# Two layers of attention on one core: v from seven block products in place of eight, and additions moved to transfers

## The chip, the cores and the metric

The kernel runs on one core of a Trainium2 chip. The core has five engines that each work through a list of their own: TensorE (PE: matrix products into PSUM), VectorE (DVE), ScalarE (ACT), GpSimd (POOL) and SyncE (SP, which only issues transfers here). They wait for each other through semaphores. The measure is the device time of one execution in microseconds (us), and lower is better.

## The reference

The reference takes 16 samples x of 256 channels by 1024 positions (32 x 32) through two layers. Each layer normalises in 16 groups and adds an attention with 4 heads of 64 channels to its input. Cut to what matters:

```python
for l in range(2):
    xf = group_norm(x)                        # per sample: (256, 1024)
    q, k, v = (W @ xf + b for W, b in ...)    # 256 x 256 weights
    sim = q_head.T @ k_head                   # (1024, 1024) for each head
    qpos = (rel_h + rel_w).T @ q_head
    attn = softmax(sim + qpos, axis=-1)
    x = x + v_head @ attn.T
```

## The kernel before

**Units and blocks.** One sample in one layer is a unit. There are 32, in the order of the list `units`, u = 0 to 31. A unit has four blocks, b = 0 to 3: pair of heads pr = 0 with query half 0 and 1, then pair pr = 1 with half 0 and 1. Blocks 0 and 2 are called the first and the second even block here, 1 and 3 the odd ones. `block(n)` writes out the program of block n. Everything is recorded in this order (`tc.manual_schedule`), and each engine works strictly through its own part of it, so a statement's place in `block` sets the order on every engine.

**One block.** For each of eight chunks j of 128 keys: `seed(blk, j)` lets VectorE write the position term of both heads into two PSUM banks (128 x 1024 values, L513; with `halves` it is two instructions of 512). `scores(blk, j)` adds q k on TensorE (S1 to S7 below are the scores of chunk 1 to 7; L549, four matmuls of 512 columns) and ScalarE takes exp into an SBUF tile p (L562). `attend` multiplies v by all eight p (L602) in two passes, called `values_of_p(0)` and `(1)`, with the first scores of the next block in between. `add_up` adds the p of a block up for the softmax's denominator: p0 + p1 is `first`, p2 comes to it by an accumulating transfer, the rest goes into `acc`. Transfers from POOL's queue with `accum_op` then fold the sums (`add_first`, `fold`, `fold_again`, `fold_stack`).

**The array.** Every large matmul uses one 64 x 64 quarter of TensorE's array. A stage has work for all four quarters at once, and comes as two stretches (`stretches`): the second adds the other half of the contraction and waits until the first is done. Each fp32 matmul shows up as two records in the trace. A round means one record on each of the four quarters.

**Banks.** PSUM's eight banks are used as four pairs, named by `ring`: ta, tb, tx, tz. In an even block tz holds q and k under construction (`qk`), and ta, tb, tx serve the seeds. tx first holds v under construction (`pv`, two stretches of 32 records), is copied out by ScalarE after S2 (`v_out`, L470) and then takes seeds; the output `po` sits in tx at the block's end.

**q, k, v.** While the blocks of one pair of heads run, q and k of the next pair (w, pr) are made: with seven products of 128 x 128 by 128 x 512 blocks in place of eight (Strassen's scheme in Winograd's form). `forms` makes the sums of weight blocks S1 to S4, `input_sums` those of the input T1 to T4 (L344, L349, L351, in a second even block). The first product stands alone (`first_product`, L360) and is woven with the first stretch of v (`woven`), since each of its stretches uses half of the array. The other six come as three pairs (`two_products`, L409). v itself is made with all eight block products, one half of the positions in each even block (`values`, L445; matmuls of 256 columns).

**The end of a block.** Six blocks later `finish` multiplies the output by 1/denominator (`normalise`, L720) and adds the bias of v and the residual (`add_residual`, L727), both on VectorE; in layer 1 SP stores the result. The norm of later units is spread over ScalarE by tables (`APPLY`, `NEXT`, `SUMS`, `SQUARES`: at which point of block b which of the 16 groups are done; L221, L296).

Of the kernel before, what the change touches and what calls it, by code (L numbers as in the profile page):

```python
# [17 lines left out]
P = 128  # L18
HALF = 512
G = 16  # L20
# [38 lines left out]
def fast_path(ctx, tc, sh, x, layers, out, W, den_all, good, flag):  # L59
# [90 lines left out]

    def taken(parts):
        for l, part in parts:
            w = {"Wq": W.form[l][:, :CC], "Wk": raw_wk(l), "Wv": W.wv[l]}[part]
            nc.scalar.copy(w.rearrange("p a c -> p (a c)"), raw_t.pop((l, part)))

    def forms(l):
# [3 lines left out]
        for to, a, b, op in (  # L160
            (S1, k0, k1, ALU.add),
            (S2, f[:, S1], f[:, A11], ALU.subtract),
            (S3, f[:, A11], k0, ALU.subtract),
            (S4, f[:, A12], f[:, S2], ALU.subtract),
# [271 lines left out]

    def values(u, g, pv, first=None):
# [4 lines left out]
        def part(t, i, cc, rs, a):  # L442
            for x, c in enumerate(QUARTERS):
# [4 lines left out]
                    W.wv[l][rs, cc, :],  # L448
# [245 lines left out]
    def reciprocals(u, pr, count=2):  # L694
# [9 lines left out]
        rden = opool.tile([P, 2 * HALF], F32, tag="rden", name=f"rden_{u}_{pr}")  # L704
# [26 lines left out]
    def add_by_dma(u, pr):  # L731
        b, l = units[u]
        xs = xt[b][:, pr, :]
        nc.scalar.activation(xs, xs, AF.Identity, bias=W.bv[l][:, pr : pr + 1])
        nc.gpsimd.dma_start(xs, outs.pop((u, pr)).rearrange("p a n -> p (a n)"), accum_op=ALU.add)

# [42 lines left out]
    APPLY = {0: (3, 7, 7, 7, 7, 7), 1: (7, 7, 7, 11, G, G)}  # L779
    NEXT = {3: (0, 0, 0, 0, 3, 3)}  # L780
    SUMS = {0: (0, 0, 0, 6, 9, 14), 1: (14, 14, 14, G, G, G)}
    SQUARES = {2: (0, 4, 5, 10, 12, G)}

    FIRST_SQUARES = {0: (2, 5, 9, 12, 12, 12)}
    FIRST_SUMS = {0: (0, 0, 0, 0, 6, 12), }
    FIRST_APPLY = {1: (0, 0, 3, 8, G, G)}

    def norms(u, b, i):
        def groups(table):
            return range(*table.get(b, (0,) * 6)[i : i + 2])  # L790
# [12 lines left out]
    def block(n):  # L803
# [18 lines left out]
        if previous and even:  # L822
            add_up(previous, 7)
        if folded and even:
            add_first(previous)
        if summed:
            fold_stack(*summed, R // 4)
        if even:
            qk = psum2(tz, f"qk_{w}_{pr}") if not plain else None
            first = None if plain else first_product(w, pr, qk)  # L830
            v, v_out = values(w, 1 - b // 2, psum2(tx, f"pv_{w}_{b}"), first)
            if n > 0:
                scores(blk, 1)
            if b == 2:
                input_sums(w, 0)
            v(0)
            norms(u, b, 0)
            if n > 0:
                seed(blk, 3, ta)
# [10 lines left out]
            add_up(blk, 1)  # L850
            v(1)
            if folded:
# [6 lines left out]
            v_out()  # L859
            if n > 0:  # L860
                scores(blk, 3)
            seed(blk, 4, tb)
            if n == 0:
                forms(0)
            if plain:
# [5 lines left out]
            products(0)  # L871
            norms(u, b, 1)
            seed(blk, 5, tx, halves=True)
# [714 lines left out]
```

## Time and profile before

| | us |
|---|---|
| time, median of 3 runs (lowest to highest) | 2478.74 (2478.73 to 2479.44) |
| the profiled execution's own time | 2479.26 |
| its span in the trace | 2477.5 |
| seeds, L513, busy | 1241.2 |
| scores, L549, busy | 1068.9 |
| attention, L602, busy | 951.6 |
| v, L445, busy | 301.3 |

The profile comes from one execution. Each row of a timeline has the start and the length in us from the span's start, the engine, the line and the operation, what is written from what, the shape, how many instructions are merged, and in brackets how long the engine had been idle and what released it. Matmuls are pipelined: the length of a row on PE reaches past the start of the next, so a stage is measured from its start to the next one's start. Rows of groups give the sum of busy time, the mean of one instruction in ns, and the idle time ahead of them. The granted clock of TensorE was 0.999 over the span.

### The profile page before, as it was taken

The page shows a single profiled execution, that of the slowest core. Times are in us where ns is not written, and L with a number is a line of the kernel's source. Part 1 is how long each engine was busy: PE and PEld are TensorE (multiplying, and loading weights), DVE is VectorE, ACT ScalarE, POOL GpSimd, SP SyncE. Part 2 cuts the span into 40 slices and gives each one's busy share as a digit, 9 for nine tenths or more (in the row PEclk, how much of TensorE's full clock was granted, in tenths as well). Part 3 has the DMA queues.
Part 4 walks back from the last instruction along what each step waited for, and adds up shares of the span by engine and source line. Part 5 has one row for each costly group of instructions (what it writes and reads, how often), then busy time and mean ns, then how long its engine had stood idle before and what let it go on. Part 6 is the DMA issues. An engine that isn't in the chain of part 4 may idle for free.

```text
span 2477.5 us, 86516 instructions
## 1 busy us (share of the span) xinstructions
PE 2467.9 (100%) x37030; PEld 1825.8 (74%) x37030; DVE 2350.6 (95%) x2815; ACT 2076.5 (84%) x4341; POOL 795.7 (32%) x942
## 2 busy tenths in 40 slices
PE   9999999999999999999999999999999999999998
PEld 5777777777777777777777777777777777777785
DVE  8899999999999999999999999999999999999998
ACT  8888888898888888888888889888888888888764
POOL 0233333333333333333333333333333333333231
PEclk9999999999999999999999999999999999999999
DMA  3655655657557566565575665665656656556564
GB/s 95 115 104 98 129 96 114 119 118 144 112 115 144 105 116 118 108 137 112 113 133 108 125 119 99 130 134 109 129 118 135 116 93 131 112 96 121 106 129 116
DMA packets 138551, 289.25 MB, mean 117 GB/s; under 512 B 55848, under 2 KB 57384, under 8 KB 138160
## 3 DMA queue, kind: packets, MB, share of 16 engines
q0 software_dynamic: 72288, 197.74, 47.3%
q1 hardware_dynamic: 65584, 85.38, 11.6%
q8 instruction: 293, 4.80, 0.8%
q14 instruction: 98, 0.80, 0.1%
q10 hardware_dynamic: 288, 0.52, 0.1%
HBM read 51.78 MB, written 17.30 MB: 28 GB/s over the span
## 4 chain that ended last, share of the span: by engine, by line
PE 98%; DVE 1%; ACT 1%; DMA 0%; issue 0%; SPq 0%; PEldq 0%; ACTq 0%
PE banks L549 36%; PE banks L602 35%; PE banks L409 13%; PE banks L445 9%; PE banks L486 2%; PE banks L360 2%; PE banks L317 0%; PE banks L240 0%; DVE banks L513 0%; DMA x<-in_x_dram 0%; ACT p L562 0%; PE banks L675 0%; ACT xn L296 0%; ACT junk L221 0%; DVE r L1121 0%
## 5 line engine op out<-in xcount | busy, mean ns | idle before, releaser
L513 DVE TENSOR_TENSOR banks<-abt 128x1024 f32<-128x1024 f32 x1207 | 1241.2, 1061 | 93.3 <-ACT p L562 49.2
L562 ACT ACTIVATE p<-banks,shift 128x1024 f32<-128x1024 f32 x898 | 981.4, 1116 | 202.5 <-PE banks L549 104.6
L549 PE MATMUL banks<-q,k 64*64 64x512 f32 x8192 | 1068.9, 590 | 0.5 <-DVE banks L513 0.4
L602 PE MATMUL banks<-p,v 64*64 64x256 f32 x16384 | 951.6, 376 | 0.0
L602 PEld LDWEIGHTS banks<-p,v 64*64 64x64 f32 x16384 | 838.5, 133 | 120.4 <-issue 39.1
L549 PEld LDWEIGHTS banks<-q,k 64*64 64x64 f32 x8192 | 466.2, 133 | 281.8 <-issue 153.7
L582 DVE TENSOR_TENSOR acc<-acc,p 128x1024 f32<-128x1024 f32 x381 | 465.2, 1221 | 4.3
L648 POOL DMA_DIRECT2D stack<-stack x310 | 308.2, 994 | 316.8 <-DMA stack<-stack 148.7
L409 PE MATMUL banks<-t,form 64*64 64x512 f32 x1984 | 399.7, 589 | 0.0
L643 POOL DMA_DIRECT2D stack<-acc x248 | 241.6, 1186 | 471.2 <-DMA stack<-acc 458.0
L445 PE MATMUL banks<-Wv,xn 64*64 64x256 f32 x3968 | 293.5, 378 | 0.0
L409 PE MATMUL banks<-xn,form 64*64 64x512 f32 x992 | 258.8, 589 | 0.0
L445 PEld LDWEIGHTS banks<-Wv,xn 64*64 64x64 f32 x3968 | 228.9, 133 | 40.2 <-PEq L199 16.8
L619 POOL DMA_DIRECT2D acc<-first x126 | 115.1, 914 | 423.1 <-DVE acc L582 224.3
L296 ACT ACTIVATE xn<-x,nshift,rstd 128x128 f32<-128x128 f32 x496 | 209.3, 500 | 30.1 <-DVE nshift L289 30.1
L221 ACT ACTIVATE junk<-x,neg 128x128 f32<-128x128 f32 x501 | 199.7, 407 | 0.0
L560 ACT ACTIVATE p<-banks,shift 128x512 f32<-128x512 f32 x252 | 159.8, 685 | 35.3 <-PE banks L549 32.3
L409 PEld LDWEIGHTS banks<-t,form 64*64 64x64 f32 x1984 | 137.8, 133 | 67.8 <-issue 41.8
L624 POOL DMA_DIRECT2D acc<-acc x124 | 103.3, 833 | 254.5 <-DMA acc<-first 251.4
L578 POOL DMA_DIRECT2D first<-p x127 | 114.1, 899 | 179.2 <-ACT abt L499 66.8
L567 DVE TENSOR_TENSOR acc<-p,p 128x1024 f32<-128x1024 f32 x128 | 156.2, 1220 | 0.4 <-DMA acc<-first 0.4
L567 DVE TENSOR_TENSOR first<-p,p 128x1024 f32<-128x1024 f32 x127 | 154.7, 1218 | 0.0
(120 smaller groups left out, 1776.6 us busy)
## 6 DMA issues: line engine op xcount, KB each, us to landing
first<-p POOLq DMA_DIRECT2D x127, 512.0 KB, 6.8
acc<-first POOLq DMA_DIRECT2D x126, 512.0 KB, 5.5
rden<-rd SPq DMA_DIRECT2D x126, 256.0 KB, 6.7
acc<-acc POOLq DMA_DIRECT2D x124, 256.0 KB, 5.9
stack<-acc SPq DMA_DIRECT2D x248, 64.0 KB, 2.9
stack<-acc POOLq DMA_DIRECT2D x248, 64.0 KB, 3.4
out_dram<-x SPq DMA_DIRECT2D x31, 512.0 KB, 2.9
x<-in_x_dram SPq DMA_DIRECT2D x30, 512.0 KB, 9.5
```

What stands on the lines that cost most here:

```text
L221: nc.scalar.activation(junk, grouped(xt[units[u][0]], g), func, accum_out=into[:, g : g + 1], **bias)
L296: nc.scalar.activation(grouped(xns[u], g), grouped(xt[units[u][0]], g), AF.Identity, bias=shift[:, g : g + 1], scale=rstd[:, g : g + 1],)
L409: yield nc.tensor.matmul(ps[c, a, :], f[rs, left[a], c0 : c0 + D], right[a][rs, :], start=(t == 0 and step == 1 and a == 1), stop=(t == 1) ...
L445: yield nc.tensor.matmul(pv[c, a, i, :], xns[u][rs, cc, j0 : j0 + D], W.wv[l][rs, cc, :], start=(t == 0 and cc == 0 and i == 0), stop=(t = ...
L513: nc.vector.tensor_tensor(ps[:, h].rearrange("p h (w y) -> p h w y", y=H), ab[:, h, :H].unsqueeze(2).to_broadcast(shape), ab[:, h, H + hal ...
L549: nc.tensor.matmul(ps[c, h, :], a[hs, j0 : j0 + D], b[hs, columns], start=bool(tag) and i == 0, stop=i == len(terms) - 1, skip_group_check ...
L562: nc.scalar.activation(p, ps, AF.Exp, bias=W.shift)
L567: nc.vector.tensor_tensor(t, probs[blk, a], probs[blk, b], ALU.add)
L582: nc.vector.tensor_tensor(accs[blk], accs[blk], probs[blk, j], ALU.add)
L602: yield nc.tensor.matmul(po[c, a, :QUART], vts[u, j // 4][rs, j % 4, c0 : c0 + D], p[rs, h, a * QUART : (a + 1) * QUART], start=(fresh and ...
L643: nc.gpsimd.dma_start(at, acc[R:D, h, :], accum_op=ALU.add)
L648: nc.gpsimd.dma_start(stack[:rows_], stack[rows_ : 2 * rows_], accum_op=ALU.add)
```

## The change

v is made with the seven products too, of weight forms that `value_forms` prepares. Its matmuls have 128 columns (`value_part`), with the input as the stationary operand. It takes three steps in two blocks. The second even block of the unit before has the first product, together with the first product of q and k (`odd_products`: each takes the half of the array that the other leaves free), and a pair (`value_pair`, step 0). The first even block of the unit itself has the two other pairs, the first of them woven with the first product of q and k. v's four blocks are put together from the banks (`bank_of(pv, a)` is one of the two, `value_block` 4 x 128 columns of v): by ScalarE's copies (c22, c11, u2 and a part), by three additions on VectorE (c22, c11, c12), and by two accumulating transfers (c22 += u2, u2 += part) on POOL's queue.

`pv` therefore keeps the pair tx until both steps are done. Seeds 3 to 6 turn on ta and tb, seed 7 goes to tx, and `po` to ta. The bias of v is added to x by ScalarE in block 3 (`add_bias`), and the residual by an accumulating transfer (`add_output`). Some additions of p, and the norm's pieces, have other places.

The first place is the first even block of a unit. PE there, before, from S2 to S7 and the attention, in the block of unit 13, pair 0, half 0 (L549 scores, L445 v, L409 pairs of products, L602 attention; the names are those of the tiles, with unit, pair, half and chunk).

```order
L549 MATMUL banks_127<-q_13_0_12239,k_13_0_12240 64x512 x4
L445 MATMUL banks_127<-Wv1_79,xn_13_11648 64x256 x16
L549 MATMUL banks_127<-q_13_0_12239,k_13_0_12240 64x512 x4
L409 MATMUL banks_127<-t_13_12162,form1_77 64x512 x2
L409 MATMUL banks_127<-xn_13_11648,form1_77 64x512 x2
L549 MATMUL banks_127<-q_13_0_12239,k_13_0_12240 64x512 x8
L409 MATMUL banks_127<-xn_13_11648,form1_77 64x512 x2
L409 MATMUL banks_127<-t_13_12162,form1_77 64x512 x2
L549 MATMUL banks_127<-q_13_0_12239,k_13_0_12240 64x512 x8
```

And now, from S2 to the start of v's third stretch (L630 scores, L457 v, L426 pairs of products):

```order
L630 MATMUL banks_127<-q_13_0_12895,k_13_0_12896 64x512 x4
L457 MATMUL banks_127<-vform1_79,t_13_12837 64x128 x16
L630 MATMUL banks_127<-q_13_0_12895,k_13_0_12896 64x512 x4
L426 MATMUL banks_127<-t_13_12837,form1_77 64x512 x2
L426 MATMUL banks_127<-xn_13_12294,form1_77 64x512 x2
L630 MATMUL banks_127<-q_13_0_12895,k_13_0_12896 64x512 x4
L457 MATMUL banks_127<-vform1_79,xn_13_12294 64x128 x2
L457 MATMUL banks_127<-vform1_79,t_13_12837 64x128 x2
```

v's matmuls are half as wide, and a third stretch of v (eight such rows) has come in behind S4. Behind it follow S5, v's fourth stretch, S6, the stretch of products that stood behind S5 before, and S7.

VectorE in the same block before, from the last addition of the block ahead to the residual (L582 and L567 additions of p, L513 seeds, L720 normalise, L727 the residual):

```order
L582 TENSOR_TENSOR acc_12_1_1_12514<-acc_12_1_1_12514,p_12_1_1_7_12478 128x1024
L513 TENSOR_TENSOR banks_127<-abt_13_0_12512 128x1024
L567 TENSOR_TENSOR first_13_0_0_12668<-p_13_0_0_0_12558,p_13_0_0_1_12633 128x1024
L513 TENSOR_TENSOR banks_127<-abt_13_0_12512 128x1024
L513 TENSOR_TENSOR banks_127<-abt_13_0_12512 128x512 x2
L513 TENSOR_TENSOR banks_127<-abt_13_0_12512 128x1024
L513 TENSOR_TENSOR banks_127<-abt_13_0_12512 128x512 x2
L720 TENSOR_TENSOR od_11_1_11467<-od_11_1_11467,rden_11_1_12461 128x1024
L727 SCALAR_TENSOR_TENSOR x_4_3665<-od_11_1_11467,bv1_85,x_4_3665 128x1024
```

And now (L594 seeds, L663 and L648 additions of p, L972 and L1016 additions for v, L806 normalise):

```order
L663 TENSOR_TENSOR acc_12_1_1_13213<-acc_12_1_1_13213,p_12_1_1_6_13167 128x1024
L594 TENSOR_TENSOR banks_127<-abt_13_0_13211 128x1024
L663 TENSOR_TENSOR acc_12_1_1_13213<-acc_12_1_1_13213,p_12_1_1_7_13177 128x1024
L594 TENSOR_TENSOR banks_127<-abt_13_0_13211 128x1024
L594 TENSOR_TENSOR banks_127<-abt_13_0_13211 128x512 x2
L972 TENSOR_TENSOR v_13_1_13327<-v_13_1_13327,banks_127 128x4x128
L594 TENSOR_TENSOR banks_127<-abt_13_0_13211 128x512 x2
L594 TENSOR_TENSOR banks_127<-abt_13_0_13211 128x1024
L1016 TENSOR_TENSOR v_13_1_13327<-v_13_0_12875,banks_127 128x4x128
L594 TENSOR_TENSOR banks_127<-abt_13_0_13211 128x512 x2
L648 TENSOR_TENSOR first_13_0_0_13476<-p_13_0_0_0_13256,p_13_0_0_1_13332 128x1024
L806 TENSOR_TENSOR od_11_1_12111<-od_11_1_12111,rden_11_1_13160 128x1024
```

Seed 4 is split, the additions for c22 and c12 stand between the seeds, p0 + p1 has moved behind seed 7, and the residual has gone.

The second place is the way from an even block into the odd one. VectorE before, from p3 + p4 of the second even block to the addition of p7 in the odd one (L433 adds into k):

```order
L567 TENSOR_TENSOR acc_13_1_0_13289<-p_13_1_0_3_13175,p_13_1_0_4_13192 128x1024
L582 TENSOR_TENSOR acc_13_1_0_13289<-acc_13_1_0_13289,p_13_1_0_5_13202 128x1024
L513 TENSOR_TENSOR banks_127<-abt_13_1_12982 128x1024
L582 TENSOR_TENSOR acc_13_1_0_13289<-acc_13_1_0_13289,p_13_1_0_6_13216 128x1024
L513 TENSOR_TENSOR banks_127<-abt_13_1_12982 128x1024 x2
L433 SCALAR_TENSOR_TENSOR k_14_0_13179<-banks_127,bk0_82,k_14_0_13179 128x512
L513 TENSOR_TENSOR banks_127<-abt_13_1_12982 128x512 x2
L513 TENSOR_TENSOR banks_127<-abt_13_1_12982 128x1024 x2
L582 TENSOR_TENSOR acc_13_1_0_13289<-acc_13_1_0_13289,p_13_1_0_7_13224 128x1024
```

And now (L450 adds into k):

```order
L648 TENSOR_TENSOR acc_13_1_0_14042<-p_13_1_0_3_13886,p_13_1_0_4_13914 128x1024
L663 TENSOR_TENSOR acc_13_1_0_14042<-acc_13_1_0_14042,p_13_1_0_5_13949 128x1024
L594 TENSOR_TENSOR banks_127<-abt_13_1_13712 128x1024
L663 TENSOR_TENSOR acc_13_1_0_14042<-acc_13_1_0_14042,p_13_1_0_6_13966 128x1024
L663 TENSOR_TENSOR acc_13_1_0_14042<-acc_13_1_0_14042,p_13_1_0_7_13977 128x1024
L594 TENSOR_TENSOR banks_127<-abt_13_1_13712 128x1024 x2
L450 SCALAR_TENSOR_TENSOR k_14_0_13891<-banks_127,bk0_82,k_14_0_13891 128x512
L594 TENSOR_TENSOR banks_127<-abt_13_1_13712 128x512 x2
L594 TENSOR_TENSOR banks_127<-abt_13_1_13712 128x1024 x2
```

The addition of p7 stands ahead of the seed of chunk 3 and not behind that of chunk 7.

ScalarE in the first odd block before, from the copy of k to the exp of chunk 5 (L560 and L562 exp):

```order
L428 COPY k_13_1_12706<-banks_127 128x512
L560 ACTIVATE p_13_0_1_2_12887<-banks_127,shift_71 128x512 x2
L562 ACTIVATE p_13_0_1_3_12895<-banks_127,shift_71 128x1024
L562 ACTIVATE p_13_0_1_4_12903<-banks_127,shift_71 128x1024
L562 ACTIVATE p_13_0_1_5_12914<-banks_127,shift_71 128x1024
```

And now (L641 and L643 exp, L238 a group's sum for the norm):

```order
L445 COPY k_13_1_13404<-banks_127 128x512
L641 ACTIVATE p_13_0_1_2_13612<-banks_127,shift_71 128x512 x2
L238 ACTIVATE junk_15_4_13616,red_15_13557<-x_6_7816 128x128
L643 ACTIVATE p_13_0_1_3_13622<-banks_127,shift_71 128x1024
L643 ACTIVATE p_13_0_1_4_13630<-banks_127,shift_71 128x1024
L643 ACTIVATE p_13_0_1_5_13641<-banks_127,shift_71 128x1024
```

One group's sum stands between the exp of chunk 2 and that of chunk 3.

The diff, cut to what was spoken of. Left out are the same rotation in the program's first and last blocks, the path that is taken only when a denominator leaves its range, `value_forms` (the sums of weight blocks for v), and the places of weights and of 1/denominator in memory.

```diff
+    def value_part(u, ps, rs, a, form, right, i, start=False, stop=False):
+        for x, c in enumerate(QUARTERS):
+            p0 = i * P + x * D
+            yield nc.tensor.matmul(
+                ps[c, a, i * P : (i + 1) * P], right[rs, p0 : p0 + D],
+                W.vform[units[u][1]][rs, form, :],
+                start=start and i == 0, stop=stop, skip_group_check=True,
+            )
+
+    def odd_products(u, pr, qk, pv):
...
+        def products(t):
+            mine, other = ((LO, HI), (HI, LO))[t]
+            for i in range(NT // 2):
+                if i < 2:
+                    c, c0 = QUARTERS[i], pr * P + i * D
+                    yield nc.tensor.matmul(
+                        qk[c, 0, :], f[other, A11, c0 : c0 + D], xb(u, 0, 0)[other, :],
+                        start=t == 0, stop=t == 1, skip_group_check=True,
+                    )
+                yield from value_part(u, pv, mine, 0, A11, xb(u, 0, 0), i, t == 0, t == 1)
+
+        return stretches(products)
+
+    def value_pair(u, step, pv, first=None):
...
+        left, right = (
+            ((S2, A12), (ts[u][:, T2], xb(u, 1, 0))),
+            ((S1, S3), (ts[u][:, T1], ts[u][:, T3])),
+            ((S4, NA22), (xb(u, 1, 1), ts[u][:, T4])),
+        )[step]
+
+        fresh = (1, 0, 2)[step]
...
+        def products(t):
+            rounds = [
+                [
+                    value_part(
+                        u, pv, rs, a, left[a], right[a], i, t == 0 and a >= fresh, t == 1
+                    )
+                    for rs, a in BANKS[t]
+                ]
+                for i in range(NT // 2)
+            ]
+            if t == 0 and first is not None:
+                yield from woven(rounds, first)
+            else:
+                for r in rounds:
+                    for p in r:
+                        yield from p
...
+    def add_bias(u, pr):
         b, l = units[u]
         xs = xt[b][:, pr, :]
         nc.scalar.activation(xs, xs, AF.Identity, bias=W.bv[l][:, pr : pr + 1])
+
+    def add_output(u, pr):
+        xs = xt[units[u][0]][:, pr, :]
         nc.gpsimd.dma_start(xs, outs.pop((u, pr)).rearrange("p a n -> p (a n)"), accum_op=ALU.add)
...
-    APPLY = {0: (3, 7, 7, 7, 7, 7), 1: (7, 7, 7, 11, G, G)}
-    NEXT = {3: (0, 0, 0, 0, 3, 3)}
-    SUMS = {0: (0, 0, 0, 6, 9, 14), 1: (14, 14, 14, G, G, G)}
-    SQUARES = {2: (0, 4, 5, 10, 12, G)}
-
-    FIRST_SQUARES = {0: (2, 5, 9, 12, 12, 12)}
-    FIRST_SUMS = {0: (0, 0, 0, 0, 6, 12), }
-    FIRST_APPLY = {1: (0, 0, 3, 8, G, G)}
+    APPLY = {0: (3, 3, 4, 5, 5, 9, 12, 12), 1: (12, 12, 12, 12, G)}
+    NEXT = {3: (0, 0, 0, 0, 3)}
+    SUMS = {0: (0, 0, 0, 0, 0, 0, 0, 4), 1: (4, 5, 7, G, G)}
+    SQUARES = {2: (0, 0, 1, 2, 4, 8, 11, G)}
...
+        def rest_of_previous():
             add_up(previous, 7)
-        if folded and even:
-            add_first(previous)
+            if folded:
+                add_first(previous)
+
+        if even and b == 2:
+            rest_of_previous()
+            input_sums(w, 0)
...
-            first = None if plain else first_product(w, pr, qk)
-            v, v_out = values(w, 1 - b // 2, psum2(tx, f"pv_{w}_{b}"), first)
+            pv = psum2(tx, f"pv_{w}_{b}")
+            if plain:
+                v, v_out = values(w, 1, pv)
+            elif b == 0:
+                new_values(w, 1)
+                v = value_pair(w, 1, pv, first_product(w, pr, qk))
+            else:
+                v = odd_products(w, pr, qk, pv)
...
-            if not plain:
+            if n > 0:
+                if b == 0:
+                    rest_of_previous()
+                seed(blk, 3, ta)
...
-                scores(blk, 2)
+                scores(blk, 2, halves=b == 0)
...
-            add_up(blk, 1)
             v(1)
+            if b == 2:
+                new_values(w, 0)
+                nc.scalar.copy(value_block(w, 0, 0), bank_of(pv, 0))
+                after_first(w, pr, qk)
+            elif plain:
+                v_out()
+            else:
+                c22, u2 = value_block(w, 1, 1), value_block(w, 0, 1)
+                nc.scalar.copy(c22, bank_of(pv, 0))
...
-            v_out()
+            seed(blk, 4, tb, halves=b == 0 and n > 0)
+            if b == 0 and not plain:
+                nc.vector.tensor_tensor(c22, c22, bank_of(pv, 1), ALU.add)
+                nc.gpsimd.dma_start(c22, u2, accum_op=ALU.add)
...
-            seed(blk, 4, tb)
+            norms(u, b, 1)
...
-            products(0)
-            norms(u, b, 1)
-            seed(blk, 5, tx, halves=True)
-            scores(blk, 4, halves=True)
-            seed(blk, 6, ta)
+                v = value_pair(w, 2 - b, pv)
+            seed(blk, 5, ta, halves=True)
+            if b == 2:
+                v(0)
+                scores(blk, 4)
+                norms(u, b, 2)
+                v(1)
+                c11 = value_block(w, 0, 0)
+                nc.vector.tensor_tensor(c11, c11, bank_of(pv, 1), ALU.add)
+                nc.scalar.copy(value_block(w, 0, 1), bank_of(pv, 0))
+                products(0)
+                norms(u, b, 3)
+                scores(blk, 5)
+                seed(blk, 6, tb)
+                products(1)
+            else:
+                products(0)
+                scores(blk, 4)
+                norms(u, b, 2)
+                if not plain:
+                    v(0)
+                scores(blk, 5)
+                seed(blk, 6, tb)
+                if not plain:
+                    v(1)
+                    c12 = value_block(w, 1, 0)
+                    part = bank_of(xns[w][:, :, :HALF], 0)
+                    nc.scalar.copy(part, bank_of(pv, 1))
+                    nc.vector.tensor_tensor(c12, u2, bank_of(pv, 0), ALU.add)
+                norms(u, b, 3)
             if folded:
                 stack_up(previous)
-            scores(blk, 5)
-            products(1)
-            po = psum2(tx, f"po_{n}")
+            po = psum2(ta, f"po_{n}")
             zeroed(po)
-            seed(blk, 7, tb, halves=True)
+            seed(blk, 7, tx, halves=True)
             scores(blk, 6)
+            if b == 0:
...
+            if not plain:
+                add_up(blk, 1)
             if before:
-                finish(*before)
+                normalise(*before)
+                add_output(*before)
+                if units[before[0]][1] == NL - 1:
+                    store(*before)
...
+            ta, tb, tx = tb, tx, ta
+            ring[:] = ta, tb, tx, tz
             seed(after, 0, ta)
...
+            if b == 0 and not plain:
+                nc.gpsimd.dma_start(u2, part, accum_op=ALU.add)
...
+            if n > 0:
+                add_up(blk, 7)
             seed(after, 3, tb)
...
-            add_up(previous, 7)
+            if n == 1:
+                add_up(previous, 7)
...
+            add_up(blk, 5)
             seed(after, 0, tb)
...
+            if b == 3 and u + 2 < NU:
+                for which in range(CC):
+                    add_bias(u, which)
             values_of_p = attend(blk, po)
             values_of_p(0)
-            if two:
-                mean_out = (norm_mean if b == 1 else norm_var)(u + 2, pm)
             scores(after, 0)
+            if two and b == 3:
+                mean_out = norm_var(u + 2, pm)
```

More of the change, by code (lines that the diff above doesn't have):

```diff
@@ L163, in forms, with value_forms @@
             (S3, f[:, A11], k0, ALU.subtract),
+            (S4, f[:, A12], f[:, S2], ALU.subtract),
+        ):
+            nc.vector.tensor_tensor(f[:, to], a, b, op)
+    def value_forms(l):
+        f, w = W.vform[l], raw_wv(l)
+        a21, a22 = (w[:, cc, P:] for cc in range(CC))
+        nc.scalar.copy(f[:, A11 : A12 + 1], w[:, :, :P])
+        nc.scalar.activation(f[:, NA22], a22, AF.Identity, scale=-1.0)
+        for to, a, b, op in (
+            (S1, a21, a22, ALU.add),
+            (S2, f[:, S1], f[:, A11], ALU.subtract),
+            (S3, f[:, A11], a21, ALU.subtract),
             (S4, f[:, A12], f[:, S2], ALU.subtract),
@@ L435, in k_half, with value_block, bank_of, new_values @@
         )
+    def value_part(u, ps, rs, a, form, right, i, start=False, stop=False):
[7 more added lines that the diff above has]
+    def odd_products(u, pr, qk, pv):
+        f = W.form[units[u][1]]
+        def products(t):
[32 more added lines that the diff above has]
+                        yield from p
+        return stretches(products)
+    def value_block(u, nh, ch):
+        return vts[u, nh][:, :, ch * P : (ch + 1) * P]
+    def bank_of(ps, a):
+        return ps[:, a, :].rearrange("p (b c) -> p b c", c=P)
+    def new_values(u, g):
+        vts[u, g] = vpool.tile([P, NT // 2, C], F32, tag="v", name=f"v_{u}_{g}")
     def values(u, g, pv, first=None):
@@ L1007, in block @@
                 stack_up(previous)
-            if two:
+            if two and b == 3:
                 mean_out()
-                if b == 3:
-                    norm_shift(u + 2)
+                norm_shift(u + 2)
             if u + 2 == NU and b == 3:
                 widen(u + 1, 1)
-            add_up(blk, 5)
             if last:
@@ L1018, in block @@
             else:
+                add_up(blk, 6)
                 seed(after, 2, tb)
-                add_up(blk, 6)
-            norms(u, b, 3)
-            values_of_p(1)
+            if two and b == 1:
+                later = []
+                values_of_p(1, 8, lambda: later.append(norm_mean(u + 2, pm)))
+                later[0]()
+                norms(u, b, 3)
+            else:
+                norms(u, b, 3)
+                values_of_p(1)
             take_out(blk, po)
@@ L1509, in __init__ @@
         self.form = [new(f"form{l}", [P, 7, sh.C]) for l in both]
-        self.wv = [new(f"Wv{l}", [P, sh.CC, sh.C]) for l in both]
+        self.vform = [new(f"vform{l}", [P, 7, P]) for l in both]
         self.bq, self.bk, self.bv = (
```

65 lines of the change are left out of this document (40 added, 25 removed).

## The prediction

> **What bounds the kernel now.** I read the page first, for the engine that sets the end.
>
> ```profile
> span 2477.5 us, 86516 instructions
> PE 2467.9 (100%) x37030; PEld 1825.8 (74%) x37030; DVE 2350.6 (95%) x2815; ACT 2076.5 (84%) x4341; POOL 795.7 (32%) x942
> ...
> PE 98%; DVE 1%; ACT 1%; DMA 0%; issue 0%; SPq 0%; PEldq 0%; ACTq 0%
> ```
>
> TensorE (PE) is the chain: 98% of it, busy 2467.9 of 2477.5 us. VectorE (DVE) is close behind, 95% busy. The waits of PE, longest first, tell whether VectorE holds it up anywhere.
>
> ```profile
> PE banks L1173 <- DVE shift L1507: 1.2, 1, 1.2
> PE banks L1187 <- DVE part L1179: 0.5, 2, 0.3
> PE banks L549 <- DVE banks L513: 0.4, 2, 0.3
> ```
>
> Two waits for a seed in 1024 scores, 0.4 us in all. So every microsecond of matmul work that goes is worth a microsecond, and every new wait of TensorE costs all of its length. The timeline of PE in the first even block of a unit gives the price of each stage, as the distance from its start to the next one's.
>
> ```profile
> 1021.23 1.07 PE L549 MATMUL banks<-q,k 64*64 64x512 f32 x8
> 1022.09 0.63 PE L360 MATMUL banks<-xn,form 64*64 64x512 f32 x2
> 1022.14 0.65 PE L445 MATMUL banks<-Wv,xn 64*64 64x256 f32 x4
> ...
> 1022.62 1.60 PE L445 MATMUL banks<-Wv,xn 64*64 64x256 f32 x22
> 1023.92 0.60 PE L360 MATMUL banks<-xn,form 64*64 64x512 f32 x2
> ...
> 1024.67 1.13 PE L549 MATMUL banks<-q,k 64*64 64x512 f32 x8
> 1025.53 2.00 PE L445 MATMUL banks<-Wv,xn 64*64 64x256 f32 x32
> 1027.26 1.13 PE L549 MATMUL banks<-q,k 64*64 64x512 f32 x8
> 1028.12 0.63 PE L409 MATMUL banks<-t,form 64*64 64x512 f32 x2
> ...
> 1028.97 1.99 PE L549 MATMUL banks<-q,k 64*64 64x512 f32 x16
> ```
>
> Scores S1 take 0.86 us, the first product woven with half of v 2.58 (1022.09 to 1024.67), S2 0.86, the other half of v 1.73, a stretch of two products 0.85 (1028.12 to 1028.97).
>
> **What v saves.** v has matmuls of 128 columns now, which no row shows. Two rows of the chain in order of time enclose them.
>
> ```profile
> 58.35 0.93 PE banks L486 x64
> 59.28 3.46 PE banks L602 x64
> ```
>
> 64 records are 16 rounds of the four 64x64 quarters: 58 ns a round at 64 columns, 216 ns at 256. By ns per column a round of 128 costs between 108 (as at 256) and 116 (as at 64). The straight line through both gives 110.5, which I take: 8 rounds, 0.884 us, for one block product.
>
> Before, a unit pays 2 x (2.58 + 1.73) = 8.62 us for v and the first product of q and k. After, the first even block (pr = 0) has the first product woven with half a pair, 0.857 + 0.884, and three more stretches of 0.884: 4.39. The second has four stretches of 0.884: 3.54. That is 7.93, so 0.69 us less in a unit and 21.4 in the 31 units that change; the ends of the range are 0.56 (17 us) and 0.77 (24 us).
>
> The Trainium skill speaks against such small matmuls: TensorE: Matmul & The Clock Gate, section Back-to-back issue gap, gives about 81 ns per sustained matmul at N = 128. By it the 224 records of v in a unit would take 18.1 us, and the kernel some 370 us more. The positions row above has 14.5 ns per record at half the columns, so I follow the row.
>
> **What it costs: the turn of a pair of banks.** Each pair of PSUM banks turns: seed (VectorE), scores (PE), exp (ScalarE), next seed. The rows of one turn, from the timelines of ACT, DVE and PEld:
>
> ```profile
> 1025.87 1.12 ACT L562 ACTIVATE p<-banks,shift 128x1024 f32<-128x1024 f32 x1 [0.25 <-PE banks L549]
> 1007.80 2.12 ACT L562 ACTIVATE p<-banks,shift 128x1024 f32<-128x1024 f32 x2
> 1005.54 1.23 DVE L513 TENSOR_TENSOR banks<-abt 128x1024 f32<-128x1024 f32 x1 [0.38 <-ACT od L663]
> 1007.36 1.30 DVE L513 TENSOR_TENSOR banks<-abt 128x512 f32<-128x512 f32 x2
> 1008.95 2.37 DVE L513 TENSOR_TENSOR banks<-abt 128x1024 f32<-128x1024 f32 x2 [0.28 <-ACT p L562]
> 1006.83 0.17 PEld L549 LDWEIGHTS banks<-q,k 64*64 64x64 f32 x4 [0.26 <-DVE banks L513]
> ```
>
> S2 starts at 1024.67 and its exp at 1025.87: 1.20. Exp takes 1.12 (the first of the pair ends at 1008.92) and the seed starts 0.03 later; the seed takes 1.23 whole or 1.30 in halves, and the weight load that waits for it starts 0.06 after its end (1006.77 to 1006.83). A turn is 3.64 us, or 3.71. Now v holds its two banks from the start of an even block until S6, so S1 to S6 turn on two pairs, where v's were free after S3. Between S(j) and S(j+2) PE then has two scores and two stretches: 0.857 x 3 + 0.884 = 3.46, or 3.48 with v in both. The turn is longer than its cover.
>
> **First even block.** (a) S3 to S5, seed in halves: 3.71 against 3.46, less some 0.05 because the second half is needed a matmul later: 0.2. (b) Seed 7 goes into v's banks: after v's last stretch ends, S6 and a product stretch are its cover, 1.71. It needs the drain of PE (0.2, as the 1.13 of x8 scores reaches 0.27 past the next stage), the addition that makes c12, 128x512 (0.70 as a half seed, and the seed waits for its end), both halves (1.30), and 0.06: 2.26, a wait of 0.52. (c) The weave: the first product's low rows were covered by two rounds of v, 0.86; two rounds are 0.44 now, and the first matmul of its high rows still waits for the low rows' last result, 0.86 + 0.2. The high half of the array has v for 0.88, then waits until about 1.08: 0.2.
>
> For (c) the Trainium skill has a harsher rule (the same page, Part 3, The mechanism): matmuls start strictly in program order. By it the high half would stand from 0.44 to 0.86 and lose 0.42, some 7 us more in the kernel. The rows of before differ: 4 + 22 records of v start before the high rows at 1023.92, where the program has 24 ahead of them.
>
> **Second even block.** S1 to S3, seed whole: 3.64 against 3.48, and v's next stretch, which adds onto the bank that the copy of c11 reads, waits for that copy, which stands behind exp 2 on ScalarE. Together 0.2.
>
> **First odd block.** Seeds 6 and 7 run as one piece, and S7 has little margin:
>
> ```profile
> 1010.62 1.99 PE L549 MATMUL banks<-q,k 64*64 64x512 f32 x16
> ...
> 1036.04 0.33 ACT L221 ACTIVATE junk<-x 128x128 f32<-128x128 f32 x1
> ...
> 1036.34 0.32 ACT L221 ACTIVATE junk<-x 128x128 f32<-128x128 f32 x1
> ```
>
> The pair of seeds at 1008.95 ends at 1011.32, S7 starts at 1010.62 + 0.86 = 1011.48: 0.16, of which 0.06 is the latency. SUMS now puts one group's sum, 0.30 from one start to the next, ahead of exp 3, and so ahead of both seeds: a wait of 0.2.
>
> **From the second even block into the odd one.** Probability 7 is added before seed 3 now, not in the odd block.
>
> ```profile
> 1080.22 1.23 DVE L513 TENSOR_TENSOR banks<-abt 128x1024 f32<-128x1024 f32 x1
> 1081.82 1.24 DVE L513 TENSOR_TENSOR banks<-abt 128x1024 f32<-128x1024 f32 x1 [0.38 <-ACT od L663]
> ...
> 1081.74 2.85 PE L549 MATMUL banks<-q,k 64*64 64x512 f32 x24
> ...
> 1022.46 2.48 DVE L582 TENSOR_TENSOR acc<-acc,p 128x1024 f32<-128x1024 f32 x2
> ```
>
> Seeds 3 and 4 stand at 1080.22 and 1081.82, S2 to S4 at 1081.74, 1082.60 and 1083.45. The addition is 1.25 (half of 2.48). It takes the 0.38 of idle time, and seed 3 moves to 1081.47, seed 4 to 1082.61, so ready at 1083.90: 0.45 late, less 0.1 that this block's VectorE work is ahead. I take 0.3; the seeds after it follow. In the first even block VectorE has 0.6 less to do (no `input_sums` there) and this costs nothing.
>
> **What is hidden.** The other terms leave PE alone if their cover holds.
>
> ```profile
> L727 DVE SCALAR_TENSOR_TENSOR x<-od,bv,x 128x1024 f32<-128x1024 f32 x62 | 79.7, 1285 | 2.2
> L734 ACT ACTIVATE x<-x,bv 128x1024 f32<-128x1024 f32 x1 | 1.1, 1142 | 0.0
> 1018.04 1.12 ACT L562 ACTIVATE p<-banks,shift 128x1024 f32<-128x1024 f32 x1 [3.21 <-PE banks L549]
> q0 software_dynamic: 72288, 197.74, 47.3%
> first<-p POOLq DMA_DIRECT2D x127, 512.0 KB, 6.8
> ```
>
> VectorE loses 79.7 us of residuals and gains 93 additions of 0.70, 65 us, and 31 split seeds of 0.17, 5 us. ScalarE gains two biases in a unit, 2.3 us, in the last block's wait of 3.21; without that cover the next exp would slip 1.1. The accumulating queue gets 62 x 0.75 of the first<-p transfers, 46 more than the some 380 of that size that fill 47.3%, so near 59%. Their landing of 6.8 us is waited for a block or more later (a v block in the second even block, some 38 us on; a residual by the next sums of that sample). I count nothing; a late landing would stand in front of an exp.
>
> **The sum.** Waits in a unit: 0.2 + 0.52 + 0.2 + 0.2 + 0.2 + 0.3 = 1.62 us, 50.2 in 31 units, against 21.4 saved: 28.8 more than the profiled execution's 2479.26, so 2508.1. The median shown, 2478.74, is 0.5 lower: **2507.6**. With each wait 0.1 less or more (0.6 in a unit, 19 us) it is 2488 to 2526.
>
> **Rivals.** Faster: seed 7 is the place, and the first half of a seed the mechanism. S7 may begin with half 0, and if the matmuls behind it go on while half 1 is added, as v's records overtook the high rows, waits (a) and (b) shrink to the chain up to half 0: (a) to nothing, (b) to under 0.1 (2.26 less 0.65 against 1.71). With (c) and the VectorE waits at their low ends the total falls under 0.5 and the time to 2458 to 2474. It decides below 0.69 of waits in a unit. For it: the overtaking. Against: the second half's wait stands in PE's own order, ahead of all that follows. Chance 0.30. No change: waits of 0.55 to 0.85 eat the saving, 2474 to 2484; 0.14. Worse: the waits in VectorE's row (95% busy) add up past 2.2 in a unit, or a landing is late: 2526 to 2540; 0.05. That small matmuls run at the page's rate: 0.01. The change doing less than it says, 128 columns at 116 ns, is only 4 us and lies in the forecast, 0.50.
>
> **Chances.** About 0.2% (5 us) can be told from no change. Faster by more 0.30, within 0.13, slower 0.57. The range is 2461 to 2522: it leaves out the fastest part of the faster rival (0.1) and the slowest cases (0.1).
>
> **What would show it.** In the new profile PE should wait for seeds some 1 us and more in a unit, at S5 and S7 of the first even block, and PE's idle time should be near 40 us. Matmuls of `value_part` should come at 110 ns a round. PE without waits for seeds, or S7 starting before its second half is there, makes the forecast wrong; so does a wait on a DMA's landing at an exp.

## The result, and the profile after

The changed kernel takes 2628.57 us (median of 4 runs, 2622.92 to 2632.78) against 2479.05 us before: 1.0599 times as long, 95% interval 1.0586 to 1.0612. The forecast was 2507.6 with a range of 2461 to 2522. The direction was right, the size was not: 150 us more, where 29 were forecast. The profiled execution took 2632.78 us.

The page of the changed kernel, its head and the chain that ended last:

```profile
span 2630.7 us, 92935 instructions
...
PE 2541.7 (97%) x40006; PEld 1647.4 (63%) x40006; DVE 2351.7 (89%) x2887; ACT 2109.1 (80%) x4373; POOL 934.3 (36%) x1064
...
DMA 8%; PE 5%; issue 2%; DVE 2%; POOL 1%; SPq 1%; ACT 0%; POOLq 0%; DVEq 0%
```

TensorE no longer fills the span, and transfers head the chain (it could be followed back through a fifth of the span only). VectorE's busy time is the same, over a longer span. The waits, with us in total, times, and the longest:

```profile
ACT od L744 <- DMA x<-od: 98.0, 35, 5.6
...
PE banks L630 <- DVE banks L594: 79.0, 40, 4.3
...
ACT junk L238 <- DMA x<-od: 22.7, 6, 4.6
```

Before, TensorE waited 0.4 us for seeds. Now it is 79.0 us in only 40 places, up to 4.3 us each, and ScalarE waits 98.0 us for the residual's transfer x<-od at the copy of `po` into od. That is not the pattern of the forecast, which had six small waits in every unit. One such place, from the timelines of POOL, ACT and PE:

```profile
1172.71 0.83 POOL L705 DMA_DIRECT2D acc<-acc  x1 [4.82 <-DMA acc<-first]
...
1174.87 2.60 POOL L973 DMA_DIRECT2D v<-v  x1
1175.67 2.71 POOL L659 DMA_DIRECT2D first<-p  x1
1176.20 3.05 POOL L824 DMA_DIRECT2D x<-od  x1
```

```profile
1187.86 0.58 ACT L744 COPY od<-banks 128x512 f32<-128x512 f32 x1 [5.59 <-DMA x<-od]
```

```profile
1183.40 2.06 PE L630 MATMUL banks<-q,k 64*64 64x512 f32 x15
1189.76 1.98 PE L630 MATMUL banks<-q,k 64*64 64x512 f32 x8 [4.30 <-DVE banks L594]
1191.52 1.06 PE L426 MATMUL banks<-xn,form 64*64 64x512 f32 x1
...
1193.23 1.58 PE L630 MATMUL banks<-q,k 64*64 64x512 f32 x8
1194.64 0.59 PE L426 MATMUL banks<-t,form 64*64 64x512 f32 x1
```

Three transfers leave POOL within 1.33 us: c22 += u2 (v<-v), p2's (first<-p) and the residual's. The queue had stood at the folds until 1172.71. The residual's lands at 1187.8, and od has three buffers: the copy of the block's `po` needs the one that this transfer reads. It waits 5.59 us, the seed that needs po's banks waits behind it, and TensorE stands for 4.30.

Then a second loss shows: behind the stand the scores from 1189.76 take 1.76 us, the products 1.71 and the next scores 1.41, all 0.86 otherwise. The table by windows has the granted clock (ahead of the DMA share) for these stretches:

```profile
1189.70:1194.60 4.90, 4.84 (x24) 1.54 (x28) 4.39 (x7) 2.80 (x5) 2.86 (x3) 0.53 0.75 89
1195.50:1200.00 4.50, 4.50 (x120) 2.77 (x116) 4.18 (x4) 4.50 (x10) 3.39 (x4) 1.00 0.64 108
```

In the trace's record of the granted clock, the changed kernel has 17 stretches of half clock, mostly 3.41 us long, which lose 35.0 us (half their length); before there is one, 3.4 us lost. The Trainium skill (TensorE: Matmul & The Clock Gate, What's actually happening) has such a drop after a window of about 3.4 us without work, and a window of it to come back. The length agrees. Here 16 idle times of TensorE, from 1.97 us on, came with a drop, though one of 2.84 was not; the 17th drop stands at the program's end, as the one of before does.

**Where in a unit the time goes.** Every exp of the program can be found in both traces (ScalarE, 8 in a block). The table has how much later each exp starts than the one ahead of it, compared with before: start less the previous exp's start, after minus before, mean of units 2 to 29, in us. Rows are the blocks, columns the chunks 0 to 7.

```
changed kernel                                     sum 5.05 a unit
b=0  -0.14  0.12 -0.56 -0.89  0.09  0.78  0.32  1.12
b=1   0.39  0.06  2.14  0.29  0.24  0.83  0.47 -0.02
b=2  -0.57  0.17 -1.70 -0.67  0.06  1.50 -0.01  0.00
b=3   0.13  0.14  0.25  0.02  0.00  0.49  0.00  0.00
without the residual's transfer (e1, below)        sum 1.53 a unit
b=0  -0.14  0.12 -0.58 -0.89  0.10  0.77  0.32  1.12
b=1   0.39  0.06 -0.06  0.30  0.00 -0.28  0.47 -0.02
b=2  -0.23  0.16 -1.69 -0.66  0.07  1.50 -0.01  0.00
b=3   0.14  0.15 -0.05  0.02  0.00  0.47  0.00  0.00
```

The 2.14 at exp 2 of b=1 is the wait for od, and the 0.83 at exp 5 mostly the half clock behind it: in the 15 of these units that have a drop there, this step is 1.0 to 2.4 us more than in e1, in the others at most 0.5.

### The profile page after: what moved, and what is told of

It is laid out like the page before. It is cut to its first block, busy times and chain, and to the rows that moved or that the text cites. A ratio compares the mean times of both kernels' runs of the same rounds, so it can differ in the third digit from the quotient of the medians.

```text
span 2630.7 us, 92935 instructions
## 1 busy us (share of the span) xinstructions
PE 2541.7 (97%) x40006; PEld 1647.4 (63%) x40006; DVE 2351.7 (89%) x2887; ACT 2109.1 (80%) x4373; POOL 934.3 (36%) x1064
## 3 DMA queue, kind: packets, MB, share of 16 engines
q0 software_dynamic: 113664, 245.46, 55.4%
## 5 line engine op out<-in xcount | busy, mean ns | idle before, releaser
L594 DVE TENSOR_TENSOR banks<-abt 128x1024 f32<-128x1024 f32 (+1 forms) x1238 | 1240.3, 1038 | 195.8 <-ACT od L744 79.9
L630 PE MATMUL banks<-q,k 64*64 64x512 f32 x8192 | 1217.4, 604 | 80.7 <-DVE banks L594 79.0
L643 ACT ACTIVATE p<-banks,shift 128x1024 f32<-128x1024 f32 x930 | 1019.2, 1114 | 236.9 <-PE banks L630 210.4
L683 PEld LDWEIGHTS banks<-p,v 64*64 64x64 f32 x16384 | 748.7, 133 | 202.5 <-issue 38.1
L630 PEld LDWEIGHTS banks<-q,k 64*64 64x64 f32 x8192 | 387.4, 134 | 472.1 <-DVE banks L594 268.6
L663 DVE TENSOR_TENSOR acc<-acc,p 128x1024 f32<-128x1024 f32 x381 | 465.6, 1222 | 10.9
L426 PE MATMUL banks<-t,form 64*64 64x512 f32 x1984 | 445.9, 602 | 0.0
L426 PE MATMUL banks<-xn,form 64*64 64x512 f32 x992 | 271.4, 616 | 0.0
L457 PE MATMUL banks<-vform,t 64*64 64x128 f32 x3968 | 245.1, 272 | 0.0
L457 PEld LDWEIGHTS banks<-vform,t 64*64 64x64 f32 x3968 | 206.2, 133 | 39.3 <-ACT v L956 25.1
L457 PEld LDWEIGHTS banks<-vform,xn 64*64 64x64 f32 x2976 | 181.1, 133 | 40.6 <-issue 29.2
L659 POOL DMA_DIRECT2D first<-p x127 | 178.5, 1405 | 78.4 <-DVE form L169 29.6
L457 PE MATMUL banks<-vform,xn 64*64 64x128 f32 x2976 | 205.1, 271 | 0.0
L238 ACT ACTIVATE junk<-x,neg 128x128 f32<-128x128 f32 x501 | 198.2, 405 | 0.0
L426 PEld LDWEIGHTS banks<-t,form 64*64 64x64 f32 x1984 | 145.2, 136 | 61.8 <-issue 15.7
L744 ACT COPY od<-banks 128x512 f32<-128x512 f32 x127 | 73.5, 579 | 137.6 <-DMA x<-od 98.0
```

The source lines that it names most:

```text
L238: nc.scalar.activation(junk, grouped(xt[units[u][0]], g), func, accum_out=into[:, g : g + 1], **bias)
L426: yield nc.tensor.matmul(ps[c, a, :], f[rs, left[a], c0 : c0 + D], right[a][rs, :], start=(t == 0 and step == 1 and a == 1), stop=(t == 1) ...
L457: yield nc.tensor.matmul(ps[c, a, i * P : (i + 1) * P], right[rs, p0 : p0 + D], W.vform[units[u][1]][rs, form, :], start=start and i == 0, ...
L594: nc.vector.tensor_tensor(ps[:, h].rearrange("p h (w y) -> p h w y", y=H), ab[:, h, :H].unsqueeze(2).to_broadcast(shape), ab[:, h, H + hal ...
L630: nc.tensor.matmul(ps[c, h, :], a[hs, j0 : j0 + D], b[hs, columns], start=bool(tag) and i == 0, stop=i == len(terms) - 1, skip_group_check ...
L643: nc.scalar.activation(p, ps, AF.Exp, bias=W.shift)
```

## The experiments

Theory A: the residual's transfer is late and od's buffer waits for it. Theory B: the queue is too full as a whole.

**e1, the residual's transfer left out.** `add_output(*before)` becomes `outs.pop(before)`.

> The changed kernel without the accumulating transfer of the residual x += od (the attention's output is not added to x; the bias still is). Theory A: this transfer lands late, the copy that takes po out waits for od's buffer, TensorE stands and its granted clock halves behind the stand. Then the waits of ScalarE for x<-od (98 us at the copy into od, 23 us at the norm's sums) are gone, the granted clock is back at 0.999 and the time falls from 2629 to between 2505 and 2530, what is left above 2479 being the waits for seeds. Theory B: the queue as a whole is too full, v's own two transfers are late as well: then it stays above 2580.

2529.9 us, clock 0.999, no wait for od. So leaving this transfer out wins 103 us against the changed kernel's profiled execution, and the rest of the change costs 49.

**e2, the residual earlier.**

```diff
+            if before:
+                normalise(*before)
+                add_output(*before)
             seed(blk, 4, tb, halves=b == 0 and n > 0)
```

> The changed kernel with normalise and the residual's transfer moved ahead of seed 4 of the even block, some 8 us earlier; nothing is left out. Theory A: the buffer of od is free in time, the wait of the copy into od falls from 98 us to under 15, granted clock above 0.996, time 2505 to 2540. Theory B (queue too full): the landing comes hardly earlier, over 2590. A VectorE addition ahead of seed 4 may cost up to 0.6 us in an even block, at most 35 us in all.

2570.26 us, more than A allows. The wait for od is gone, but another one has come, since p2's transfer lands later now (8.9 us after its issue, 7.1 in the changed kernel) and the exps wait for its buffer:

```profile
ACT p L643 <- DMA first<-p: 39.2, 33, 4.5
```

In b=2 the step at exp 3 went from -0.66 to 0.52: normalise delays seed 4.

**e3, the residual on VectorE.** `finish(*before)` in place of the two calls, `add_bias` gone.

> The changed kernel with bias and residual added on VectorE again, as before (one 1.28 us instruction behind normalise, no bias on ScalarE); v's two transfers stay. Theory A: no wait for x<-od is left, granted clock 0.999, time 2500 to 2540. Theory B: the v transfers load the queue enough for late landings, over 2580.

2595.77 us at a clock of 1.0, with no wait for x<-od: both missed. The steps say why: 1.08 at exp 0 of b=3 (0.14 in e1), 0.82 at exp 0 of b=1 (0.39), 0.55 at its exp 5 (-0.28). VectorE has no room for the residuals beside v's additions.

**e4, the transfer in the kernel before.** `normalise`, `add_output` and `add_bias` there.

> The kernel before, with this one part of the change: bias on ScalarE in block 3, residual by the accumulating transfer at its old place. Theory A: the transfer alone is late against od's third buffer, 2530 to 2600 with a granted clock under 0.996. If it takes v's transfers in the queue as well (a mixture of A and B): under 2495, with the copy into od waiting for less than 15 us.

2495.45 us, beside 2480.64 of the kernel before: 15 us, no wait for od. So A alone is not enough; something in the changed kernel makes this transfer late. The 15 us themselves stand in six units, where the sums for the norm of the same sample ask for x 2.4 to 2.6 us after the transfer's issue; in the other units the exps come as before, within 0.3 us a unit:

```profile
ACT junk L221 <- DMA x<-od: 21.9, 6, 4.3
```

The issues of transfers have the median us to landing at the end, first of e4, then of the changed kernel:

```profile
x<-od POOLq DMA_DIRECT2D x61, 512.0 KB, 5.9
```

```profile
x<-od POOLq DMA_DIRECT2D x61, 512.0 KB, 9.8
```

**e5, c22's transfer behind the residual's.** The line `nc.gpsimd.dma_start(c22, u2, ...)` moved behind `store(*before)`.

> The changed kernel with the transfer c22 += u2 recorded behind the residual's transfer and not ahead of it (nothing left out). Theory C: the residual's transfer is late because the queue hands over three transfers at once (c22's 256 KB, p2's 512 KB, then the residual's 512 KB) behind the waits of the folds: without c22's ahead it lands about 2 us earlier (median 9.8 down to 7.5 to 8.5), the wait of the copy into od falls from 98 to 20 to 60 us and the time to 2560 to 2600. If c22's place does not matter: within 10 us of 2629.

2585.28 us, as theory C has it; landing (8.6) and wait for od (62.7) are just above its 8.5 and 60.

**e6, od in two halves.** Two tiles, two instructions of `normalise`, two transfers.

> The changed kernel with od as two tiles of one half each (same memory), normalise in two instructions of 512 columns, and the residual's transfer in two of 256 KB, half 0 first (nothing left out). Theory A/C: the buffer that the copy waits for is free after the first of the two, 2 to 4 us sooner, so its wait falls from 98 to under 40 us; 2535 to 2585. VectorE pays 0.2 us a unit pair. If the wait is not for the buffer: no change.

2606.39 us, a miss. The wait fell to 54.9 us only: both halves stand behind p2's transfer, and the first, which the copy waits for, lands 8.8 us after its issue, the second 10.0 (medians).

**e11, a fourth buffer.** `bufs=4` for od; to make room, the test of the denominators' range at the end covers an eighth of the blocks.

> The changed kernel with four buffers for od in place of three, all transfers and their order as they are; for the room, the check of the denominators' range at the end covers an eighth of the blocks that it covered (three VectorE instructions, the output is complete). Theory A: it is the buffer that makes the late landing cost time, so the copy into od waits for nothing, the granted clock is 0.999 and the time comes within 15 us of e1_no_residual's 2529.9 although every transfer still runs (2530 to 2545). Theory B (a full queue costs time by itself, wherever it is waited for): over 2575.

2621.39 us: theory A, as far as it lays the loss to this buffer alone, fell here. od waits for no transfer any more, and others do:

```profile
ACT p L643 <- DMA first<-p: 32.4, 16, 3.9
...
ACT junk L238 <- DMA x<-od: 32.0, 6, 6.7
```

Exps wait for p2's buffer, and the norm's sums for x. A late transfer finds someone; the buffer was only the first.

**e13 and e14, what makes it late.** e13 leaves out both transfers of v. e14 puts p0 + p1 of an even block, and with it p2's transfer, back to where it was:

```diff
+            if not plain:
+                add_up(blk, 1)
             v(1)
...
             scores(blk, 6)
             if b == 0:
                 products(1)
-            if not plain:
-                add_up(blk, 1)
```

> The changed kernel without v's two accumulating transfers (c22 and u2 lack these additions); the residual's transfer and the place of p2's stay. Theory V: v's transfers fill the queue, as the residual's alone cost the kernel before only 15 us: back to 2540 to 2560, copy into od waiting under 25 us. Theory P: it is the residual's transfer standing right behind p2's (first<-p, 512 KB each, issued within a microsecond): then about as e5_v_later, 2575 to 2600.

> The changed kernel with p0 + p1 of an even block at its old place, ahead of seed 4, so that p2's transfer is issued some 6 to 8 us ahead of the residual's; nothing is left out. Theory P: the residual's transfer lands in 6 to 8 us in place of 9.8, the copy into od waits under 40 us, and 2560 to 2590 comes out, less or more the addition's new place in VectorE's row (0.2 to 0.5 us a block, up to 30 us). Theory V: landing hardly faster, 2610 to 2650.

e13: 2548.88 us, the time of theory V, with a wait for od of 29.9 where it had under 25, and a landing of 8.1. e14: 2527.35 us, with nothing left out, better than either theory. It is the pile of three: taking v's out helps much, taking p2's away from the residual's settles it. The changed kernel itself shows the same: its residuals land a median 10.3 us after their issue in the first even block, where c22's transfer is in the pile, and 8.4 in the second, where it is not (14 of 30 landings told by the trace there). POOL in e14, and its wait and landing:

```profile
1125.45 0.87 POOL L659 DMA_DIRECT2D first<-p  x1 [1.73 <-DVE banks L594]
...
1131.75 2.27 POOL L975 DMA_DIRECT2D v<-v  x1
1133.83 1.10 POOL L824 DMA_DIRECT2D x<-od  x1
```

```profile
ACT od L744 <- DMA x<-od: 2.6, 2, 1.4
```

```profile
x<-od POOLq DMA_DIRECT2D x61, 512.0 KB, 6.0
```

p2's transfer is issued 8.4 us ahead of the residual's, not 0.5, and landing is back at 6.0. e14 moves a second thing: with p0 + p1 gone from ahead of normalise, the residual's transfer is issued some 1.1 us sooner against the copy, which ScalarE reaches a median 8.6 us after the issue in the first even block, 7.4 in the changed kernel. The landing there went from 10.3 to 7.1, so it is the larger part; no run takes the two apart. The addition's place in VectorE's row costs 0.37 at exp 4 of b=2 (0.44 against 0.07 in e1) and saves 0.46 at exp 5 of b=3.

**The terms of the forecast, without the residual's transfer.** Three runs on e1's base.

e10, the addition for c12 behind seed 7:

```diff
-                    nc.vector.tensor_tensor(c12, u2, bank_of(pv, 0), ALU.add)
...
             seed(blk, 7, tx, halves=True)
+            if b == 0 and not plain:
+                nc.vector.tensor_tensor(c12, u2, u2, ALU.add)
```

> As e1_no_residual (2529.9), and the addition that makes c12 runs behind seed 7 and reads no bank of v (v's part is left out of c12). The forecast put 0.52 us a unit on seed 7 behind c12 in v's banks; the lags of e1_no_residual say 0.65 (0.26 at exp 7 and 0.39 at the next exp 0). With the addition (0.70) away seed 7 can start as PE has drained: 2510 to 2518. If the halves of the seed hide it, as the faster rival has it: within 4 us of 2530.

2515.62 us: 14.3 less than e1, 0.46 a unit. At exp 7 of b=0 the step goes from 1.12 to 0.51; 0.57 of it returns at exp 5 of b=1, and 0.36 of that is won again at the next exp 0. The seed does wait for that addition (0.70 long) or for v's bank that it reads, which e10 takes away together, and its halves don't hide it.

e9, the norm's sum: `SUMS = {..., 1: (4, 4, 6, G, G)}`.

> As e1_no_residual (2529.9), with no group's sum ahead of exp 3 of the first odd block (table SUMS (4, 4, 6, G, G)). The forecast put 0.2 us a unit on that sum: 2522 to 2526; the lags of e1_no_residual there (0.30 at exp 3 and 0.47 at exp 6, less 0.30 taken back at exp 5) say 0.2 to 0.45, so down to 2516. If the sum is hidden: 2530.

2520.44 us, 9.5 less, 0.31 a unit.

e7, p7 of b=2 added in b=3 again.

> Without the residual's transfer as in e1_no_residual (2529.9), and probability 7 of the second even block added in the odd block again, as before the change. The forecast put 0.3 us a unit on this addition; the lags of e1_no_residual point to 0.5 (a step of 0.48 at exp 5 of the second odd block): 2513 to 2521. If those lags come from elsewhere (the shared VectorE row): within 4 us of 2530.

2550.73 us, 21 more in place of 9 to 17 less. The step at exp 5 of b=3 is gone (0.00), as the forecast's mechanism has it, but 1.08 stands at exp 0 of the next unit:

```profile
PE banks L630 <- DVE banks L250: 29.7, 31, 1.0
```

The odd block's VectorE row, which has p5's addition earlier now, has no room for it: TensorE waits 31 times for the norm's bank.

**Parts together.** e8 has e5, e6, e7 and e9 in one, e12 has e11, e5 and e9, e15 has e14 and e9.

> Complete kernel: the changed one with the halves of e6_split, c22's transfer behind the residual's, p7 added in the odd block (as in e7) and one group's sum moved from ahead of exp 3 to a later place of the odd block (table SUMS (4, 4, 6, G, G)). If the parts add up: 2530 less 15 (p7) less 7 (sum) and up to 20 for what is left of the residual: 2505 to 2530, so still slower than before, since some 1.1 us of waits in the first even block stay.

> As e11_four_od, with c22's transfer behind the residual's (e5) and no group's sum ahead of exp 3 of the odd block (e9). If the parts add up, e11's time less 8 to 12: 2518 to 2535, still 40 us over the kernel before, by the waits for seeds that stay. If late landings find another place to be waited for (probability buffers, the norm's sums): no gain over e11.

> Complete kernel: e14_first_early (2527.4) with no group's sum ahead of exp 3 of the first odd block, as in e9, which gained 9.5 us without the residual. If the two are apart: 2515 to 2521, so 1.4% to 1.7% over the kernel before. If the sum's later place meets VectorE's new row: 2527 or more.

e8: 2587.48 us, e12: 2562.18, both misses: e8 carries e7's loss, and in e12 p2's late landing still holds exps up (24.9 us). e15: 2522.6 us (median of 4, 2519.8 to 2524.89), just over the 2515 to 2521 expected, 1.0173 times the kernel before (1.0156 to 1.0190). It is the best form of the change that ran, 4% faster than the changed kernel, and still slower than before; 4.8 us under e14's single run is too little, with that spread, to call e9's term shown in it.

## Why the forecast was wrong

**What was right.** PE bounded the kernel, so that v's saving and every new wait count in full. v's matmuls came as priced:

```profile
997.45 1.11 PE L630 MATMUL banks<-q,k 64*64 64x512 f32 x8
...
1000.06 1.43 PE L630 MATMUL banks<-q,k 64*64 64x512 f32 x8
...
1003.54 1.40 PE L630 MATMUL banks<-q,k 64*64 64x512 f32 x8
...
1005.27 0.59 PE L630 MATMUL banks<-q,k 64*64 64x512 f32 x1
```

From S1 to S2, scores and the weave, are 2.61 us (0.857 + 0.857 + 0.884 = 2.60 without a wait); from S4 to S5, scores and a stretch of v, 1.73 (1.74). By these the saving of 0.69 a unit stands. The figure of the Trainium skill for small matmuls (TensorE: Matmul & The Clock Gate, Back-to-back issue gap), by which the kernel would take some 370 us more, does not hold for this form: the 8 rounds behind S4 took 0.87 us.

**The waits for seeds**, from e1's steps, each less what the moved stages explain. In b=0, S2 and S3 should come 0.84 and 0.85 sooner, and S5, S6 and S7 0.88, 0.03 and 0.86 later; in b=2, S2 and S3 1.70 and 0.85 sooner, S4 and S5 0.03 and 1.74 later:

| term | forecast | measured |
|---|---|---|
| (a) S3 to S5 turn, b=0 | 0.2 | 0.29 (exp 6, 0.32) |
| (b) seed 7 behind c12, b=0 | 0.52 | 0.65 (0.26 at exp 7, 0.39 at the next exp 0) |
| (c) weave | 0.2 | 0.2 (0.26 at exp 2, 0.04 less at exp 3) |
| b=2 | 0.2 | 0.26 (0.16 and 0.19 at exp 1 and 3, 0.24 less at exp 5, 0.14 at the next exp 0, and 0.02 of small ones) |
| b=1 | 0.2 | 0.24 (0.30 and 0.47, 0.28 less at exp 5, 0.23 less at the next exp 0, 0.02 of small ones) |
| b=2 to 3 | 0.3 | 0.57 |

They add up to 2.2 against 1.62, so 1.53 over the saving against 0.93. The step that was mis-sized most is the last, VectorE's row at p7, at half. These terms alone give 2529.9 (e1) where the forecast said 2507.6. Only three were taken out in runs, the sum of b=1 (e9), (b) (e10) and p7 (e7); the others are read from the steps. The sign that the forecast named for them, TensorE idle for near 40 us, did not come: in e1 it waits 2.7 us for seeds. It is the weight loads that wait, 205.9 us (80.9 before), and a stage then runs on in pieces:

```profile
PEld banks L630 <- DVE banks L594: 205.9, 446, 1.7
...
PE banks L630 <- DVE banks L594: 2.7, 5, 0.8
```

(a) to (c) were each within 0.13. Of the faster rival's mechanism only the start appeared, which the forecast had named as a sign against itself: S7 begins with the first half of its seed. The gain did not come, as the second half's wait is paid (e10).

```profile
1171.72 1.26 PE L630 MATMUL banks<-q,k 64*64 64x512 f32 x5
...
1172.80 0.60 PE L630 MATMUL banks<-q,k 64*64 64x512 f32 x3
```

Three of S7's records start 1.08 us after the first.

Three sums of the forecast do not come out; none bears on what failed. By 116 and 108 ns a round, the ends of v's saving are 0.34 and 0.85 us a unit, not 0.56 and 0.77. The wait (b) is 2.26 - 1.71 = 0.55, not 0.52. And the new transfers equal 93 of p2's, not 46; the share of near 59% is that of 93, and it came: 55.4% of the longer span.

**The step that failed** stands under "What is hidden": "Their landing of 6.8 us is waited for a block or more later (a v block in the second even block, some 38 us on; a residual by the next sums of that sample). I count nothing". Two things in it were wrong. The first to wait for the residual's transfer is, in most units, not the sample's sums but the next user of od's buffer: in the kernel that hardly waits its copy starts 7.9 to 9.4 us after the issue (e14, median 9.3). In six units it is the sums, but a few us behind the issue and not a block or more (e4: 2.4 to 2.6; 22.7 us of waits in the changed kernel). And 6.8 us was the median landing of p2's transfers in the kernel before, which had no transfer of a residual or of v's beside them; the share of 59% said nothing of three transfers within 1.33 us. The order of VectorE that was shown ahead of the forecast had the cause in it: p0 + p1 moved behind seed 7, right ahead of normalise, and p2's transfer moves with it. I costed that addition on VectorE and not the transfer that it issues. The loss is 103 us in the profiled execution: 79.0 of TensorE's waits for seeds against 2.7 in e1, and some 29 of half clock (35.0 less 2.6 at the program's end and 3.1 that fell into the stands), together 106; the rest is not worked out. The rival "worse" named a late landing, but at 2526 to 2540 and a chance of 0.05, with no price for the stall or for the clock behind it.

## What to carry to other kernels

A transfer that takes work off an engine holds its source until it lands: ask who needs that buffer next, and how far on. Cost a moved instruction with the transfers that it triggers, and look at what stands within a few us of them in the same queue; a queue's mean share doesn't show a pile. Where a stall of TensorE passes some 2 us, as here, count the half clock behind it too.

## What the runs showed of the hardware

A transfer of 512 KB that adds to its target landed 5.9 us after its issue (median) with p2's some 6 us ahead of it (e4), 8.4 with p2's 512 KB within 1 us ahead, and 11.6 in the place shown, behind two others (768 KB) issued within 1.33 us before; of two halves of 256 KB in its place the first landed after 8.8 us (e6). A stand of TensorE of 4.30 us was followed by two stages at half speed and a third at 1.41 us for 0.86: 2.3 us lost on top.
